# A second pair of states per tile turned on TensorE and scaled on ScalarE, and one of GpSimd's groups given to VectorE

## The chip, the cores and the metric

The kernel runs on one core of one Trainium2 chip. The metric is the device time of one execution in microseconds. A core has five engines with a queue each: TensorE (PE, with its weight loads shown apart as PEld), VectorE (DVE), ScalarE (ACT), GpSimd (POOL) and SyncE (SP, which issues most DMAs here). Each takes its instructions in order; they wait for each other through semaphores. All data is float32.

## The reference

An image tensor x of shape (4, 192, 128, 128) goes through two layers, each x + layer(group_norm(x)). Layer 1 is a convolution with fractional and ordinary Fourier transforms and is not touched. Layer 2 is a selective state-space block over the 16384 pixels of each image, read as a sequence of tokens with 192 channels. Its core, with 384 inner channels d and 16 states s:

```python
dt = softplus(einsum('blr,dr->bld', dt, dt_proj_w) + dt_proj_b)
A = -exp(A_log)                                   # (384, 16)
def step(hcar, inp):
    dt_t, B_t, C_t, u_t = inp
    dA = exp(dt_t[..., None] * A)
    hnew = hcar * dA + (dt_t * u_t)[..., None] * B_t[:, None, :]
    y_t = sum(hnew * C_t[:, None, :], axis=-1)
    return hnew, y_t
```

Ahead of it stand a layer norm, an input projection (to xs and z), a causal convolution over four tokens and silu; u is its result, and dt, B and C are projections of u. Behind it come y + u * Dp, a gate with silu(z), and an output projection.

## The kernel before

Layer 1 takes the first 1500 us. Layer 2 (`layer1` in the code, L504) cuts the 4 x 16384 tokens into 128 chunks of T = 512. A chunk has NJ = 3 tiles of 128 inner channels and NS = 16 states, taken in pairs (G = 2): NG = 8 groups per tile, 24 steps k per chunk, with tile j = k // 8 and group sg = k % 8. The loop over steps is `for pos, (n, k) in enumerate(order)` (L992); the order of the instructions is the order in which this loop writes them (a manual schedule), and each engine's queue follows it.

One state of one tile needs, for 512 tokens on 128 partitions:

- the decay exp(dt * A), by ScalarE (`decay`, L800). For groups of GpSimd it goes into a PSUM bank `op`, three states ahead (`decay_there`); for all others into one of four SBUF buffers `da`, four such states ahead (`early`);
- the input (dt * u) * B. There are three ways. GpSimd makes it for both states of a group in one operation (`inputs`, L828, tile `db`, written two steps ahead, in the queue before the `hc` of that step). VectorE makes it per state (`product`, L820), from a PSUM copy `dp` of dt * u (`dtu_copy`, L783, on ScalarE, once per tile at sg = 5) into one of the three `op` banks. Or TensorE and ScalarE do: TensorE turns dt * u so that tokens lie on partitions (`turned`, L834, four transposes of 128x128 into a `ps` bank); B is then one number per partition, so ScalarE scales it with eight activations per pair (`scale_pair`, L844, tile `dbT`, two buffers); TensorE turns it back (`turned_back`, L855, four transposes per state, into an `op` bank);
- the scan over 512 tokens, by VectorE (L869), two per step, into `h` (three buffers);
- h * C for both states, by GpSimd (L882, tile `hc`, five buffers); the sum over states by TensorE, which transposes and accumulates into `py` (`sums`, L895, three steps later; `add_skip`, L909, adds u * Dp).

At the end of a tile ScalarE copies py out (`evacuate`, L904), TensorE turns it back (`turn`, L919), and VectorE applies the gate (L924). `finish` (L933, L939) does the output projection for the chunk before.

In the same loop the *front* of later chunks goes on (`front`, a generator that advances once per step; pieces marked MID stand between the two scans of a step, pieces marked LATE behind them). For the prediction these of its lines matter: L610 to L658, the layer norm (L640 is a square root on ScalarE into `rs`, L643 its reciprocal on VectorE, L645 a transposition, L649 a copy `rows`, L653 a broadcast of the rows by TensorE, L658 the product on VectorE); L664 the input projection; L682 the convolution; L690 and L694 silu; L729 `xd`; L740, L745 and L749 dt and dt * u; L758 `bT`, the copy of B turned, which the scaling reads. Exp, silu, softplus and square root lie in different activation tables, hence ten ACT_TABLE_LOAD per chunk.

PSUM has 8 banks: three `ps`, one `dp`, three `op`, one `py`.

Which way a group goes is set by these lines:

```python
BY_POOL = ((1, 4, 7), (1, 4, 7), (1, 7))
BY_PE = 6
EARLY = 14
```

So per chunk 8 of the 24 groups are GpSimd's, 3 TensorE's and 13 VectorE's.

## Time and profile before

| | |
|---|---|
| median of 3 runs | 11592.89 us (11590.45 to 11595.39) |
| profiled execution | 11590.68 us, span 11588.6 us, mean granted clock 0.931 |
| L869 scans, DVE | 6144 in layer 2, 1263 ns each |
| L820 products, DVE | 3328, 671 ns |
| L882 hc, POOL | 3072, 2374 ns |
| L828 db, POOL | 1024, 2369 ns |
| L800 decays, ACT | 4096 of 722 ns, 2048 of 689 ns |
| L844 scaling, ACT | 3072, 371 ns (822 us busy together) |
| ACT_TABLE_LOAD of L800, ACT | 636, 1283 ns |

How to read it: durations are those of single instructions. Instructions of one engine overlap a little, so the distance from one start to the next is shorter than the duration (a 671 ns product starts 0.59 us ahead of the next instruction). Idle time stands in brackets before an instruction, with what ended it; the name given there is the last event by the profile, and where that event is long past, it was another. GpSimd's spans are rough. The granted clock is TensorE's. Steady chunks are alike, so one of them, near 6041 us, is read in detail.

### The profile page before, as it was taken

To read this page: it belongs to the slowest core of one execution; us is meant where nothing else is said; L and a number is where in the kernel's file an instruction comes from. 1 tells how busy PE (TensorE), PEld (TensorE's weight loads), DVE (VectorE), ACT (ScalarE), POOL (GpSimd) and SP (SyncE) were. 2 spreads that over 40 slices of the span, in tenths; PEclk is the share of its full clock that TensorE was granted. 3 is DMA by queue.
4 is the path that set the end of the run, shared out by engine and by line. 5 is a ranking of instruction groups with operands and counts; after the bars stand their busy time and mean duration, and the time that the engine had idled before them with its cause. 6 is when DMAs were issued, how large, how long until landed. Compare 5 with 4: busy or idle time off the path is not lost.

```text
span 11588.6 us, 153548 instructions
## 1 busy us (share of the span) xinstructions
PE 9794.3 (85%) x50570; PEld 6612.4 (57%) x50570; DVE 10751.8 (93%) x11584; ACT 8608.4 (74%) x14436; POOL 10072.1 (87%) x4598
## 2 busy tenths in 40 slices
PE   4777888888888888888888888888888888888887
PEld 2444356655656665655665665665655666566565
DVE  5565679999999999999999999999999999999999
ACT  2322168888888888888888888888888888888886
POOL 0000079999999999999999999999999999999999
PEclk8888789999999999999999999999999999999998
DMA  8787734434434434433433443443443343344343
GB/s 209 203 221 202 195 99 126 120 108 127 126 103 128 126 107 122 126 112 117 126 118 110 126 125 104 127 127 104 124 126 111 118 126 116 113 126 123 106 127 97
DMA packets 1339384, 1494.09 MB, mean 129 GB/s; under 512 B 903474, under 2 KB 954359, under 8 KB 1338071
## 3 DMA queue, kind: packets, MB, share of 16 engines
q1 hardware_dynamic: 1318102, 1421.34, 42.5%
q0 software_dynamic: 13312, 50.34, 1.4%
q10 hardware_dynamic: 7168, 12.59, 0.3%
q8 instruction: 398, 6.52, 0.2%
q14 instruction: 404, 3.30, 0.1%
HBM read 1325.19 MB, written 155.32 MB: 128 GB/s over the span
## 4 chain that ended last, share of the span: by engine, by line
DVE 32%; ACT 23%; PE 22%; issue 14%; POOL 6%; DMA 2%; DVEq 0%; SPq 0%; POOLq 0%; ACTq 0%
DVE h L869 23%; DVE op L820 7%; PE py L895 6%; ACT da L800 6%; POOL hc L882 4%; ACT op L800 4%; ACT L800 2%; ACT dbT L844 2%; PE py L909 2%; PE ps L664 2%; PE pr L471 2%; ACT dt L745 1%; POOL db L828 1%; PE ps L682 1%; PE op L855 1%
## 5 line engine op out<-in xcount | busy, mean ns | idle before, releaser
L882 POOL TENSOR_TENSOR hc<-h,bc 128x1024 f32<-128x1024 f32 x3072 | 7195.2, 2374 | 95.7 <-DVE h L869 93.7
L869 DVE TENSOR_TENSOR_SCAN h<-da,carry,op 128x512 f32<-128x512 f32 x3968 | 4932.9, 1263 | 0.0
L895 PE MATMUL py<-ident,hc 128*128 128x128 f32 x24576 | 3346.1, 283 | 604.5 <-ACT yt L904 368.3
L895 PEld LDWEIGHTS py<-ident,hc 128*128 128x128 f32 x24576 | 2941.5, 147 | 1589.7 <-issue 701.4
L800 ACT ACTIVATE da<-dt,c_A_log 128x512 f32<-128x512 f32 x4096 | 2828.1, 722 | 626.3 <-DVE h L869 620.1
L869 DVE TENSOR_TENSOR_SCAN h<-op,carry,db 128x512 f32<-128x512 f32 x1984 | 2508.4, 1264 | 86.0 <-issue 82.0
L828 POOL TENSOR_TENSOR db<-dtu,bc 128x1024 f32<-128x1024 f32 x1024 | 2425.6, 2369 | 6.3 <-DMA bc<-dbc 6.3
L820 DVE TENSOR_TENSOR op<-dp,bc 128x512 f32<-128x512 f32 x3328 | 2232.6, 671 | 32.1 <-ACT dp L783 32.1
L800 ACT ACTIVATE op<-dt,c_A_log 128x512 f32<-128x512 f32 x2048 | 1400.3, 689 | 896.4 <-DVE h L869 894.0
L664 PE MATMUL ps<-s,c_wiT 96*128 96x512 f32 x3072 | 1452.3, 595 | 2.6 <-DVE s L658 2.6
L682 PE MATMUL ps<-xs,dcw 128*128 128x512 f32 x3072 | 1424.4, 593 | 0.4 <-ACT xs L677 0.4
L933 PE MATMUL ps<-yg,c_woT 128*96 128x512 f32 x1536 | 712.1, 600 | 186.5 <-DVE xm L939 186.5
L800 ACT ACT_TABLE_LOAD x636 | 816.0, 1283 | 11.6 <-DVE h L869 0.3
L844 ACT ACTIVATE dbT<-ps,bT 128x128 f32<-128x128 f32 x3072 | 822.0, 371 | 0.0
L682 PEld LDWEIGHTS ps<-xs,dcw 128*128 128x128 f32 x3072 | 533.5, 190 | 432.3 <-issue 431.7
L664 PEld LDWEIGHTS ps<-s,c_wiT 96*128 96x128 f32 x3072 | 526.1, 191 | 379.4 <-issue 376.1
L477 POOL DMA_DIRECT2D xmid<-xt x64 | 42.6, 666 | 789.8 <-DVE xt L475 783.2
L933 PEld LDWEIGHTS ps<-yg,c_woT 128*96 128x96 f32 x1536 | 241.0, 163 | 553.8 <-issue 307.6
L633 PE MATMUL ps<-ones,xs 96*128 96x1 f32 x2048 | 292.7, 273 | 287.2 <-ACT dt L745 282.3
L909 PE MATMUL py<-ddp,u 128*128 128x128 f32 x3072 | 520.1, 326 | 0.0
L749 POOL TENSOR_TENSOR dtu<-dt,u 128x512 f32<-128x512 f32 x384 | 478.6, 1284 | 29.6 <-ACT dt L745 29.6
L909 PEld LDWEIGHTS py<-ddp,u 128*128 128x128 f32 x3072 | 487.6, 241 | 0.0
(172 smaller groups left out, 10247.2 us busy)
## 6 DMA issues: line engine op xcount, KB each, us to landing
bc<-dbc SPq DMA_DIRECT2D x1024, 1024.0 KB, 5.9
xt<-in_x SPq DMA_DIRECT2D x192, 768.0 KB, 9.6
xmid<-xt POOLq DMA_DIRECT2D x64, 768.0 KB, 7.1
xm<-xmid SPq DMA_DIRECT2D x128, 384.0 KB, 3.5
carry<-h SPq DMA_DIRECT2D x3072, 1.0 KB, 1.9
out<-xm SPq DMA_DIRECT2D x128, 384.0 KB, 3.3
d<-x ACTq DMA_DIRECT2D x64, 192.0 KB, 6.9
df<-u SPq DMA_DIRECT2D x16, 512.0 KB, 4.9
```

What stands on the lines that cost most here:

```text
L664: nc.tensor.matmul(pp, wiT[:, t, m * 128 : (m + 1) * 128], s[:, t, :], start=t == 0, stop=t == 1)
L682: nc.tensor.matmul(pc, dcw[:, j, k, :], xs[:, j, k : k + T], start=k == 0, stop=k == 3)
L749: nc.gpsimd.tensor_tensor(dtu[j], dt[j], u[j], ALU.mult)
L800: nc.scalar.activation(da, got[n]["dt"][j], AF.Exp, scale=A[:, j, st : st + 1])
L820: nc.vector.tensor_tensor(dbs[s], g["dp"], g["bc", k % NG][:, 0, q, :], ALU.mult)
L828: nc.gpsimd.tensor_tensor(db, _bc(g["dtu"][j], 1, G), g["bc", sg][:, 0], ALU.mult)
L844: nc.scalar.activation(t[:, blk, :], g["tu", j][:, blk, :], AF.Identity, scale=g["bT"][:, blk, q : q + 1])
L869: nc.vector.tensor_tensor_scan(h[:, q, :], das.pop(s), dbs.pop(s) if db is None else db[:, q, :], 0.0 if ch == 0 else g["before"][:, j, st ...
L882: nc.gpsimd.tensor_tensor(hc, h, g["bc", sg][:, 1], ALU.mult)
L895: nc.tensor.matmul(py[:, blk, :], hc[:, q, blk * 128 : (blk + 1) * 128], ident, start=first, stop=sg == NG - 1 and q == G - 1 and blk == T ...
L909: nc.tensor.matmul(got[n]["py", j][:, blk, :], got[n]["u"][j][:, blk * 128 : (blk + 1) * 128], ddp[:, j, :], start=False, stop=False, skip ...
L933: nc.tensor.matmul(po[0:CH], woT[:, j, t * CH : (t + 1) * CH], g["yg", j], start=j == 0, stop=j == NJ - 1,)
```

## The change

Group 3 of each tile joins group 6 on the way by TensorE and ScalarE. GpSimd loses group 4 of the middle tile (step 12), which VectorE then takes by products. Per chunk GpSimd has 7 groups, TensorE 6, VectorE 11. The turned dt * u of a tile serves both of its pairs; the third tile is turned twice. `TURNED` says at which step which tile is turned, `SCALED` at which step which pair is scaled: at step 0 behind the step's late pieces, elsewhere between the two scans. `bT` now holds all 16 states.

```diff
-    BY_POOL = ((1, 4, 7), (1, 4, 7), (1, 7))
-    BY_PE = 6
-    EARLY = 14
+    BY_POOL = ((1, 4, 7), (1, 7), (1, 7))
+    BY_PE = 3, 6
     MID, LATE = "mid", "late"
+
+    TURNED = {0: 0, 9: 1, 15: 2, 19: 2}
+    SCALED = {0: (0, 3), 3: (0, 6), 9: (1, 3), 11: (1, 6), 16: (2, 3), 19: (2, 6)}
...
-            g["bT"] = tp.tile([128, T // 128, G], F32, name="bT")
-            nc.scalar.copy(
-                g["bT"],
-                bt.rearrange("p (k c) -> p k c", c=128)[:, :, 96 + BY_PE * G : 96 + (BY_PE + 1) * G],
-            )
+            g["bT"] = tp.tile([128, T // 128, NS], F32, name="bT")
+            nc.scalar.copy(g["bT"], bt.rearrange("p (k c) -> p k c", c=128)[:, :, 96 : 96 + NS])
...
-            if s in turns and states[s][1] % NG != BY_PE:
+            if s in turns and states[s][1] % NG not in BY_PE:
...
-        def scale_pair(n, j):
+        def scale_pair(n, j, sg):
 
             g = got[n]
-            for q in range(G):
-                t = g["dbT", j, q] = scp.tile([128, T // 128, 128], F32, name="dbT", bufs=2)
+            for st in range(sg * G, (sg + 1) * G):
+                t = g["dbT", j, st] = scp.tile([128, T // 128, 128], F32, name="dbT", bufs=2)
...
-            if at < len(states) and states[at][1] % NG == BY_PE:
+            if at < len(states) and states[at][1] % NG in BY_PE:
...
-                if sg == BY_PE - 1:
+                if sg + 1 in BY_PE:
                     turned_back(G * (pos + 1))
...
-                if k == EARLY or sg == LAG - 1 and j < NJ - 1:
-                    turned(n, NJ - 1 if k == EARLY else j)
+                if k in TURNED:
+                    turned(n, TURNED[k])
...
                 def between():
                     go_on(parts, MID)
-                    if sg == LAG and j < NJ - 1:
-                        scale_pair(n, j)
+                    if k in SCALED and k:
+                        scale_pair(n, *SCALED[k])
...
                 go_on(parts, LATE)
-                if k == EARLY:
-                    scale_pair(n, NJ - 1)
+                if k == 0:
+                    scale_pair(n, *SCALED[k])
```

## The prediction

> **What bounds the kernel now.** First the page's busy line, then the busy time in a steady stretch of layer 2 (columns PE, PEld, DVE, ACT, POOL, granted clock, DMA share, GB/s).

> ```profile
> PE 9794.3 (85%) x50570; PEld 6612.4 (57%) x50570; DVE 10751.8 (93%) x11584; ACT 8608.4 (74%) x14436; POOL 10072.1 (87%) x4598
> ```
> ```profile
> 6000.00:8000.00 2000.00, 1732.14 (x9391) 1199.54 (x9390) 1968.67 (x2090) 1639.06 (x2772) 1985.66 (x893) 0.95 0.40 119
> ```

> GpSimd is 99.3% busy, VectorE 98.4%; ScalarE and TensorE have 18% and 13% left. Counted so, whatever leaves both saturated engines is won. So next the order of events within one chunk of 512 tokens (24 steps k of one pair of states; tiles j = k // 8). ScalarE's timeline:

> ```profile
> 2194.39 0.59 ACT L783 COPY dp<-dtu 128x512 f32<-128x512 f32 x1 [0.76 <-DVE op L820]
> ...
> 2272.90 0.59 ACT L783 COPY dp<-dtu 128x512 f32<-128x512 f32 x1 [0.76 <-POOL hc L882]
> ...
> 6041.22 0.59 ACT L783 COPY dp<-dtu 128x512 f32<-128x512 f32 x1 [0.76 <-POOL hc L882]
> ...
> 6050.80 2.12 ACT L844 ACTIVATE dbT<-ps,bT 128x128 f32<-128x128 f32 x8
> ...
> 6062.51 0.56 ACT L904 COPY yt<-py 128x512 f32<-128x512 f32 x1
> ...
> 6066.35 0.26 ACT L640 ACTIVATE rs<-ps,eps 128x4 f32<-128x4 f32 x1
> ```

> The copy of dp for the third tile (k=13) starts every 78.507 us: (6041.22 - 2272.90)/48. I call its start T0. From T0, ScalarE runs without a gap for 22.5 us (silu, softplus, four table loads, eight L844, the yt copy). VectorE and GpSimd in the same chunk:

> ```profile
> 6047.08 1.28 DVE L869 TENSOR_TENSOR_SCAN h<-op,carry,db 128x512 f32<-128x512 f32 x1 [0.67 <-issue]
> ...
> 6068.27 0.16 DVE L643 RECIPROCAL rs<-rs 128x4 f32<-128x4 f32 x1
> ...
> 6073.05 1.22 DVE L658 TENSOR_TENSOR s<-s,ps 96x1024 f32<-96x1024 f32 x1 [0.51 <-PE ps L653]
> ...
> 6106.00 1.25 DVE L869 TENSOR_TENSOR_SCAN h<-op,carry,db 128x512 f32<-128x512 f32 x1
> ```
> ```profile
> 6075.63 2.36 POOL L882 TENSOR_TENSOR hc<-h,bc 128x1024 f32<-128x1024 f32 x1 [0.59 <-DVE h L869]
> ...
> 6103.44 2.40 POOL L828 TENSOR_TENSOR db<-dtu,bc 128x1024 f32<-128x1024 f32 x1
> ```

> VectorE stands still twice per chunk, 1.2 us together: at k=15, where the scan starts 0.09 us after ScalarE's decay (6046.32 + 0.67), and at L658, which waits for the row broadcast of the front (yt, L895/L909, L664, L645, rows, L653). GpSimd waits once, for the scan after L658, and then runs 13 operations unbroken until db of group 9 is ready at about 6105.8, 0.2 us before the scan that reads it.

> So one chunk is three lengths: **A**, T0 to L658, 31.83 us, set by ScalarE and then TensorE; **B**, L658 to group 9's scan, 32.95 us, where VectorE and GpSimd end level; **C**, from there to the next T0, 13.72 us, VectorE alone. Sum 78.50.

> **The change part by part.**

> VectorE loses L820 products: groups 3, 11, 19 go to TensorE (six), group 12 comes from GpSimd (two). A product lasts 671 ns, but its start-to-start cost is 0.59 us (6040.46 to 6041.04): 4 x 0.59 = 2.34 us per chunk. The pairs fall out at k=2, k=10 and k=18, the new pair stands at k=11.

> GpSimd loses db of group 12: one of 2369 ns, 2.32 us start to start. If nothing else ended anything, a chunk would be 2.3 to 2.4 us shorter.

> ScalarE gets three more sets of eight L844. One set takes 1.99 us from its start to the next instruction (6050.80 to 6052.79); the upper end is 8 x the 371 ns mean, 2.97. I take 1.99, the same instruction in the same place. Together 6.0 us per chunk, into 78.5 - 64.4 = 14 us of idle time. The bT copy grows from 8 to 64 columns: between its 0.14 us and the 0.57 of a 128x512 copy; I take 0.2. Two decays change target (722 against 689 ns): 0.07.

> TensorE gets 24 L855 and, since the third tile is turned twice, four L834: 7 x 0.44 us = 3.1 us (0.9 each at half clock), into some 10 us of waiting. Its sums queue behind each L855, which waits for a scan; the sums release hc buffers, of which there are five, so GpSimd does not feel it. Each pair's L855 must be done before its scan. Walked through, the tightest is group 3's second (behind a convolution that waits for two xs copies, now after a set of L844), about 0.2 us early; VectorE would wait for GpSimd some steps later anyway. The second turning of tile 2 holds one of three `ps` banks until T0+23.8; L664 of the next chunk's front, which takes it, comes at 24.8 or later. Issued DMAs are the same on SP; GpSimd's queue issues none here.

> Now the three lengths.

> *A.* The set for group 19 replaces the old one of tile 2, only behind xd instead of before it: yt stays at T0+21.3. The set for group 22 now stands at k=19, right behind yt and in front of bT, the table load and rs. Before, rs was done at T0+25.4 and VectorE asked at T0+27.05. After: 20.05 (end of the L800 load, 6061.27 - 6041.22) + two decays 1.24 + yt 0.47 + set 1.99 + two decays 1.24 + bT 0.2 + load 1.29 + rs 0.3 = T0+26.8. VectorE, 1.17 us earlier through k=18, asks at T0+25.85 and stands still for about 1 us. That gain is gone. Then k=21 (2.36), L924 (0.58), a scan (1.18): VectorE asks for L658's operand at T0+31.1. Meanwhile ScalarE does load 1.3, two decays 1.24, dp 0.6, rows 0.2 (T0+30.1), and TensorE L653, 1.1: T0+31.3. A shrinks from 31.8 to 31.3.

> *B.* The scan behind L658 ends at T0+33.6; 13 GpSimd operations at 2.319 us ((6105.78 - 6075.63)/13) are the same 13 as before. db of group 9 comes at T0+64.0, its scan at 64.15. VectorE would be there at 63.1 (pair at k=2 gone) and waits at groups 7 and 9. B keeps 32.8.

> *C.* The pair saved at k=10 returns at k=11: 13.72 as before.

> Sum 77.95, 0.55 us less than 78.507. Over 127 intervals 70 us. The profiled execution took 11590.7 us (span 11588.6), 2 us under the median 11592.9: 11590.7 - 70 = 11521 us.

> The floor, with nothing late in A: GpSimd's hc of k=12 ends at T0+1.8 at the earliest (its scan ends with C); seven operations later, at 18.1, come the three L749 (3.7 us), 18 operations more bring db of group 9 at 63.5, plus C: 77.3. So at most 1.2 us per chunk, 11437.

> [...] Granted clock around the yt copy:

> ```profile
> 6060.00:6061.00 1.00, 1.00 (x9) 1.00 (x9) 1.00 (x2) 1.00 (x1) 1.00 (x2) 0.68 0.00 0
> ...
> 6067.00:6068.00 1.00, 1.00 (x9) 0.99 (x8) 1.00 (x2) 0.99 (x2) 1.00 (x1) 0.91 1.07 274
> ```

> Half clock lasts from 6060.36 to 6067.18 (by the shares 0.68 and 0.91 of these slices), 6.83 us, in every chunk at the same place (T0+19.1), and it slows exactly the work behind yt. In early chunks it began at T0+20.5 (1664.0) and the chunk took 79.19; T0+19.33 (1899.5) gave 78.61, T0+19.23 (1978.0) gave 78.56. 78.507 is 23 times 3.413, half the slow time: the chunk is locked to the clock's own period.
> [...]

> **Rivals.**
> *Full gain:* the balance decides, 76.1 us per chunk, 11285 to 11437 us. For it: 99.3% and 98.4%. Against: A and C hold nothing that the change shortens.
> *Locked again:* the slow time stays behind yt and A stretches until the chunk is 23 periods: 11590, no change. For it: the lock; against: the two L855 of group 19 fill the gap before L633, whose 2.4 us of waiting precede the slow time.
> *ScalarE too late (slower):* the set at k=19 delays rs, and VectorE's reciprocal stands in order before the scans, so A grows one for one. From 0.55 us beyond my figure the change loses; with 2.97 per set A is 1 us longer, 0.4 us per chunk over before: 11645.

> **How the numbers follow.** Forecast case 0.48, full gain 0.07, locked 0.18, ScalarE too late 0.27. The likeliest gives 11521, its own range 11475 to 11565. Leaving out the full gain and the worse part of the slower case, 11450 to 11640. Within 0.2% (23 us), what a measurement here can tell from no change: 0.18; faster 0.55; slower 0.27.

> **What would show it.** L820 at 2816 instead of 3328, L828 at 896, L844 at 6144. A new wait of the reciprocal on L642's rs of about 1 us per chunk; VectorE waiting for GpSimd's db at groups 7 and 9; GpSimd idle 2 us per chunk, before hc of k=12 and k=22; ScalarE near 91% busy. dp copies at k=13 77.9 us apart and no longer at a fixed place of the slow clock. I am wrong if rs or an L855 is later than walked here, or if the chunk stays at 78.507.

## The result and the profile after

The changed kernel takes 11584.31 us (median, 11580.53 to 11592.76), the kernel before, beside it, 11588.52 us; the ratio is 0.9997, 95% interval 0.9988 to 1.0006. That is no change, where 11521 was forecast. The profiled execution has a span of 11590.8 us.

The page's busy line, and the steady stretch of layer 2 (columns PE, PEld, DVE, ACT, POOL, granted clock, DMA share, GB/s):

```profile
PE 10615.0 (92%) x54154; PEld 7007.7 (60%) x54154; DVE 10503.1 (91%) x11072; ACT 9334.7 (81%) x17508; POOL 9823.7 (85%) x4470
```
```profile
6000.00:8000.00 2000.00, 1895.96 (x10107) 1279.08 (x10105) 1919.13 (x1988) 1784.58 (x3381) 1936.76 (x868) 0.96 0.41 120
```

The work did move. VectorE fell from 98.4% to 96.0%, GpSimd from 99.3% to 96.8%, ScalarE rose from 82% to 89%. None of it became time. What VectorE waited for in 4000 to 8000 us, 51 chunks (us in total, times, longest):

```profile
DVE rs L645 <- ACT rs L642: 58.3, 51, 2.0
DVE h L869 <- PE op L855: 45.1, 85, 1.3
DVE h L869 <- issue: 34.8, 51, 0.9
DVE h L869 <- POOL db L827: 14.6, 57, 0.8
DVE s L660 <- PE ps L655: 8.4, 51, 0.3
```

Before, two waits filled this list, at k=15 ("issue") and at L658:

```profile
DVE h L869 <- issue: 33.3, 50, 1.0
DVE s L658 <- PE ps L653: 27.1, 51, 1.0
```

The new ones, for rs, for op and for db, are 2.3 us per chunk together, as long as the four products that VectorE lost. One chunk, the lines that answer to those of the prediction; first ScalarE's timeline, then VectorE's and GpSimd's:

```profile
6047.48 0.59 ACT L782 COPY dp<-dtu 128x512 f32<-128x512 f32 x1 [0.20 <-issue]
...
6068.86 0.56 ACT L904 COPY yt<-py 128x512 f32<-128x512 f32 x1
6069.32 2.17 ACT L843 ACTIVATE dbT<-ps,bT 128x128 f32<-128x128 f32 x8
...
6074.13 0.26 ACT L642 ACTIVATE rs<-ps,eps 128x4 f32<-128x4 f32 x1
...
6125.91 0.59 ACT L782 COPY dp<-dtu 128x512 f32<-128x512 f32 x1
```
```profile
6074.43 0.18 DVE L645 RECIPROCAL rs<-rs 128x4 f32<-128x4 f32 x1 [0.99 <-ACT rs L642]
6078.91 1.22 DVE L660 TENSOR_TENSOR s<-s,ps 96x1024 f32<-96x1024 f32 x1 [0.16 <-PE ps L655]
6095.11 1.28 DVE L869 TENSOR_TENSOR_SCAN h<-da,carry,op 128x512 f32<-128x512 f32 x1 [0.84 <-PE op L855]
6111.86 1.28 DVE L869 TENSOR_TENSOR_SCAN h<-op,carry,db 128x512 f32<-128x512 f32 x1 [0.17 <-POOL db L827]
6120.41 1.28 DVE L869 TENSOR_TENSOR_SCAN h<-da,carry,op 128x512 f32<-128x512 f32 x1 [0.20 <-PE op L855]
```
```profile
6109.43 2.40 POOL L827 TENSOR_TENSOR db<-dtu,bc 128x1024 f32<-128x1024 f32 x1
```

T0 is 6047.48. A ends at L660, 6078.91: 31.43. Group 9's scan starts at 6111.86, so B is 32.95, and C, to 6125.91, is 14.05. The sum is 78.43. Over many chunks it is not: from 6047.48 to 11386.02 there are 68, of 78.508 us in the mean, the 78.507 of before. Two things have to be explained, then: why a chunk is 78.43 and not 77.95, and why the mean is 78.51 and not 78.43.

The second shows when chunks are set in a row (start of the chunk, its length, then where slow-clock stretches begin, counted from T0, and how long they last; worked out from the dp copies and the granted clock):

```
4712.68  78.43   15.6: 3.4 us   32.7: 3.4 us
4791.11  78.46   15.7: 3.4 us   32.7: 3.4 us
4869.57  78.42   15.7: 3.4 us   32.8: 3.4 us
4947.99  78.21   15.8: 3.4 us
5026.20  79.18   12.7: 6.8 us   33.2: 3.4 us
5105.38  78.42   15.4: 3.4 us   32.5: 3.4 us
```

The slow stretches of the steady chunks last 3.413 us or a whole multiple of it (4000 to 11300 us: 158 of 3.41 and 14 of 6.83 here; 6 of 3.41, 90 of 6.83 and 3 of 13.65 before), and the starts of all stretches in a trace, 283 here and 181 before, lie whole multiples of 3.4133 us apart, to 0.02 us; I call 3.413 us a window of the clock. 23 windows are 78.507. A chunk of 78.42 is 0.085 short of that, so the stretches move later in the chunk, from T0+15.4 to T0+15.8. Then the window ahead is slow too, the clock is slow for 6.8 us from T0+12.7, and that chunk takes 79.18. After that it begins anew, and the mean stays at 23 windows. That the windows hold the mean there is read from such rows; the runs that take the slow time away, below, test it.

The slow time also bears on the first question. The chunk at 4947.99 has no stretch near T0+32 and takes 78.21. In the 14 chunks of this kind between 4000 and 11300 us (of 93), C is 13.81 and not 14.05: TensorE reaches group 11's L855 at T0+72.05 there, and at T0+72.29 in the chunks with the stretch, since it comes out of the stretch late and has 0.4 us of idle time on the way to catch up, against 1.4 us in the 14. The wait of 0.20 us at 6120.41 above is what VectorE sees of it; in the 14 chunks it is 0.01. So some 0.25 of the 78.43 is slow time that lies 40 us ahead of the wait.

### The profile page after: what moved, and what is told of

It reads as the page before. It is cut to its first block, busy times and chain, and to the rows that moved or that the text cites. A ratio compares the mean times of both kernels' runs of the same rounds, so it can differ in the third digit from the quotient of the medians.

```text
span 11590.8 us, 163663 instructions
## 1 busy us (share of the span) xinstructions
PE 10615.0 (92%) x54154; PEld 7007.7 (60%) x54154; DVE 10503.1 (91%) x11072; ACT 9334.7 (81%) x17508; POOL 9823.7 (85%) x4470
## 4 chain that ended last, share of the span: by engine, by line
PE 35%; DVE 28%; ACT 23%; issue 11%; DMA 2%; POOL 1%; DVEq 0%; SPq 0%; ACTq 0%; POOLq 0%
DVE h L869 18%; PE ps L666 8%; ACT da L799 7%; PE py L895 7%; PE ps L684 6%; DVE op L819 5%; PE ps L933 3%; ACT dbT L843 3%; ACT L799 3%; PE op L855 3%; ACT op L799 2%; PE pr L471 2%; ACT s L612 2%; ACT L692 1%; ACT L642 1%
## 5 line engine op out<-in xcount | busy, mean ns | idle before, releaser
L882 POOL TENSOR_TENSOR hc<-h,bc 128x1024 f32<-128x1024 f32 x3072 | 7195.0, 2366 | 342.6 <-DVE h L869 338.2
L869 DVE TENSOR_TENSOR_SCAN h<-da,carry,op 128x512 f32<-128x512 f32 x4216 | 5227.0, 1267 | 115.2 <-PE op L855 110.9
L895 PEld LDWEIGHTS py<-ident,hc 128*128 128x128 f32 x24576 | 2963.8, 147 | 787.8 <-issue 716.3
L895 PE MATMUL py<-ident,hc 128*128 128x128 f32 x24576 | 3360.5, 283 | 25.7 <-POOL hc L882 12.4
L799 ACT ACTIVATE da<-dt,c_A_log 128x512 f32<-128x512 f32 x4352 | 3008.5, 728 | 356.9 <-DVE h L869 349.4
L869 DVE TENSOR_TENSOR_SCAN h<-op,carry,db 128x512 f32<-128x512 f32 x1736 | 2203.2, 1269 | 116.7 <-issue 83.6
L827 POOL TENSOR_TENSOR db<-dtu,bc 128x1024 f32<-128x1024 f32 x896 | 2146.2, 2395 | 6.4 <-DMA bc<-dbc 6.4
L819 DVE TENSOR_TENSOR op<-dp,bc 128x512 f32<-128x512 f32 x2816 | 1897.8, 674 | 32.1 <-ACT dp L782 32.1
L843 ACT ACTIVATE dbT<-ps,bT 128x128 f32<-128x128 f32 x6144 | 1656.8, 379 | 11.8 <-PE ps L833 11.6
L799 ACT ACTIVATE op<-dt,c_A_log 128x512 f32<-128x512 f32 x1792 | 1222.3, 683 | 548.0 <-DVE h L869 546.5
L855 PE MATMUL op<-ident,dbT 128*128 128x128 f32 x6144 | 1084.1, 297 | 102.2 <-DVE h L869 78.3
L855 PEld LDWEIGHTS op<-ident,dbT 128*128 128x128 f32 x6144 | 795.1, 152 | 528.5 <-ACT dbT L843 149.1
L742 PE MATMUL ps<-xd,c_dtT 12*128 12x512 f32 x768 | 443.6, 662 | 99.4 <-ACT dbT L843 76.0
```

What stands on the lines that cost most here:

```text
L799: nc.scalar.activation(da, got[n]["dt"][j], AF.Exp, scale=A[:, j, st : st + 1])
L819: nc.vector.tensor_tensor(dbs[s], g["dp"], g["bc", k % NG][:, 0, q, :], ALU.mult)
L827: nc.gpsimd.tensor_tensor(db, _bc(g["dtu"][j], 1, G), g["bc", sg][:, 0], ALU.mult)
L843: nc.scalar.activation(t[:, blk, :], g["tu", j][:, blk, :], AF.Identity, scale=g["bT"][:, blk, st : st + 1],)
L855: nc.tensor.transpose(db[:, blk * 128 : (blk + 1) * 128], t[:, blk, :], ident)
L869: nc.vector.tensor_tensor_scan(h[:, q, :], das.pop(s), dbs.pop(s) if db is None else db[:, q, :], 0.0 if ch == 0 else g["before"][:, j, st ...
```

## The experiments

Each is timed beside the kernel before, and ratios are to it. "Undisturbed" means the commonest chunk in the trace without a long slow stretch in A.

### Which group GpSimd gives up

```diff
-    BY_POOL = ((1, 4, 7), (1, 7), (1, 7))
+    BY_POOL = ((1, 7), (1, 4, 7), (1, 7))
```

> The changed kernel, but the group that GpSimd gives up is group 4 of the first tile (k=4) and not of the middle tile (k=12). All engine totals are those of the changed kernel. Theory of three lengths (A: T0 to the front's product, B: from there to group 9's scan, C: from there to the next T0): GpSimd's unbroken row in B is 12 operations and not 13, VectorE has 1.17 us more there and sets it at 32.9 us; C loses the products of group 12 (1.17 us) but the scan of group 11 then waits 0.6 us longer for TensorE's transposes; A stays 31.4. Sum about 78.0 us per chunk, 11535 us (11500 to 11560). Engine totals: no difference to the changed kernel, 11584. Clock lock: the chunk stays at 78.507 on average, 11588.

Measured: 11583.96 us, ratio 0.9997 (0.9988 to 1.0006). Undisturbed 78.44, every sixth or seventh chunk longer, mean 78.50. Not even the undisturbed chunk fell: C fell by 0.34 and B rose by as much, to 33.29 (32.96 in the chunks without a stretch near T0+32). Its trace shows what took the two products' place, TensorE's turned state of group 11:

```profile
6189.86 1.28 DVE L869 TENSOR_TENSOR_SCAN h<-da,carry,op 128x512 f32<-128x512 f32 x1 [1.06 <-PE op L855]
```

### The two parts of the change alone

TensorE and ScalarE's part alone is the changed kernel with the old line:

```diff
-    BY_POOL = ((1, 4, 7), (1, 7), (1, 7))
+    BY_POOL = ((1, 4, 7), (1, 4, 7), (1, 7))
```

> The second pair on TensorE and ScalarE alone; GpSimd keeps all eight groups. Three lengths: A 31.4, B 32.95 (GpSimd's row unchanged), C loses the products of group 12 and gains a longer wait for the transposes, 13.4; but GpSimd has 77.9 us of work per chunk, so 78.0 to 78.4 us, 11525 to 11575. Engine totals: GpSimd bound as before, 11588. ScalarE too late: above 11600, with waits of the reciprocal well over 1 us.

Measured: 11589.58 us, ratio 1.0000 (0.9991 to 1.0010). Chunks of 77.8, 78.9, 78.7 and 78.6 by turns. Four of them are 92 windows, so the mean is 78.50 again, with a quite different shape: in the three longer ones A is 32.3 to 32.5, with 6.8 us of slow clock ahead of yt.

GpSimd's group alone is the kernel before with one line changed:

```diff
-    BY_POOL = ((1, 4, 7), (1, 4, 7), (1, 7))
+    BY_POOL = ((1, 4, 7), (1, 7), (1, 7))
```

> The kernel before with one of GpSimd's groups (k=12) given to VectorE and nothing else. Three lengths: C grows by a pair of products, 1.17 us, A and B stay: 79.7 us per chunk, 11735 us. Engine totals: VectorE 78.3 us busy and 1.2 us of waits, 79.5 us, 11715. Clock lock: if the chunk is held at a multiple of the clock's 3.413 us it would stay at 78.507; with VectorE longer than that the lock must break.

Measured: 11725.2 us, ratio 1.0119 (1.0102 to 1.0136). Undisturbed 79.29 = A 31.41, B 32.96, C 14.92. C grew by 1.20, which is two products of 0.59; A and B kept their length although GpSimd had one operation less. The op that GpSimd gave up lay in the length that VectorE alone sets. The mean is 79.64, three chunks being 70 windows.

### Filling TensorE's time ahead of the slow stretch, in the kernel before

```diff
-            for j in range(NJ):
+            for j in [*range(NJ)] * 3:
                 rows = slice(32 * j, 32 * j + RANK)
                 nc.tensor.matmul(d[j], dtT[rows, :], xd[rows, :], start=True, stop=True)
```

> The kernel before with the three dt projections (L740) computed three times over into the same banks, 12 more passes of 512 columns per chunk, which fill TensorE's gap ahead of L633; the result is the same. Clock lock: no slow time behind the yt copy, so the row broadcast is no longer late, the chunk leaves 78.507 and falls to what GpSimd (77.9 us busy) and VectorE (77.1 plus 0.7 of waiting for a decay) allow: 77.9 to 78.1 us, 11520 to 11550 us, with slow time gone or elsewhere. If the clock has no part in it: 78.5 us and 11588, or more by the added work.

Measured: 11604.87 us, ratio 1.0014 (1.0004 to 1.0023). It went the wrong way: some chunks of 78.10, some of 80.1 to 81.8, and for the most part the old 78.507. This miss led to the cause. The granted clock in two windows in a row, and TensorE in the first of them:

```profile
6060.12:6063.53 3.41, 3.40 (x24) 1.72 (x25) 3.41 (x4) 3.39 (x6) 3.41 (x2) 1.00 0.19 27
6063.53:6066.94 3.41, 3.41 (x19) 3.41 (x18) 3.41 (x5) 3.38 (x5) 3.41 (x3) 0.50 0.04 0
```
```profile
6060.13 2.85 PE L740 MATMUL ps<-xd,c_dtT 12*128 12x512 f32 x18 [1.59 <-ACT xd L729]
```

TensorE is busy for 3.40 of the 3.41 us of a window, and the clock is halved behind it. What fills the window are matmuls of 12 rows. A little less of them, and the clock stays whole, with TensorE as busy as before:

```profile
7084.13:7087.54 3.41, 3.41 (x25) 1.73 (x26) 3.41 (x4) 3.39 (x6) 3.41 (x2) 1.00 0.16 20
7087.54:7090.96 3.42, 2.75 (x25) 2.52 (x24) 3.42 (x5) 3.39 (x5) 3.42 (x3) 1.00 0.06 5
```
```profile
7083.98 2.85 PE L740 MATMUL ps<-xd,c_dtT 12*128 12x512 f32 x18 [1.59 <-ACT xd L729]
```

The 12-row matmuls begin 0.15 us ahead of this window and have 2.70 us of it; the rest are L895's transposes. The trace holds 75 windows with over 2.6 us of 12-row matmuls (4000 to 11300 us, at full clock, all but one busy throughout). The 13 with less than 2.80 us of them are followed by full clock, those with more by half clock, and at 2.80 (to 0.01) both occur. So in this run it is not idle time that halves the clock.

### Convolution behind the turned state, and both moves together

In the changed kernel, a `yield LATE` moves the convolution matmuls of the first and third tile behind L855 in TensorE's queue:

```diff
+            yield LATE
             c0 = psum()
             conv(0, c0, 0)
...
             conv(2, c2, 0)
             yield
+            yield LATE
             conv(2, c2, 1)
```

> The changed kernel with two pieces of the front's convolution (first half for tile 0 at k=2, second half for tile 2 at k=10) moved on TensorE's queue behind the transposes of groups 3 and 11 that stood behind them. Three lengths: the wait of group 11's scan (0.28 us with its restart) goes out of C; the wait at group 3 goes too but GpSimd's row in B still sets the time there. 78.42 falls to 78.14, about 35 us under the changed kernel, 11550. Engine totals or clock lock: no difference, 11584.

Measured: 11581.91 us, ratio 0.9994 (0.9985 to 1.0002). Chunks of 78.13 and 78.90 by turns, two of them 46 windows. The undisturbed chunk fell by 0.3 as the lengths said (C is 13.75); the time did not.

With group 4 of the first tile given up as well:

> The same two pieces moved and the group taken from GpSimd at k=4 and not at k=12. Three lengths: A 31.4, B 32.9 set by VectorE, C 12.8: 77.2 us per chunk, 11420 us (11400 to 11460). Engine totals: as the changed kernel, 11584. Clock lock: 11588.

Measured: 11495.19 us, ratio 0.9918 (0.9905 to 0.9932). Undisturbed 77.08, with others of 78.3 (A 32.6 in place of 31.42, with 6.8 us of slow clock in it). Five chunks are 114 windows, so the mean is 77.81. The mean has left 78.507, but 0.7 us per chunk is still lost to slow time.

### The third tile's second pair taken back

The changed kernel with group 19 on VectorE again and the set for group 22 back at k=14:

```diff
-    BY_PE = 3, 6
+    BY_PE = (3, 6), (3, 6), (6,)
...
-    TURNED = {0: 0, 9: 1, 15: 2, 19: 2}
-    SCALED = {0: (0, 3), 3: (0, 6), 9: (1, 3), 11: (1, 6), 16: (2, 3), 19: (2, 6)}
+    TURNED = {0: 0, 9: 1, 14: 2}
+    SCALED = {0: (0, 3), 3: (0, 6), 9: (1, 3), 11: (1, 6), 14: (2, 6)}
```

> The changed kernel with the second pair in the first two tiles only; the third tile is turned once at k=14 as before, and VectorE takes group 19 by products again, 1.17 us more for VectorE, 2 us less for ScalarE per chunk. Three lengths: A is 31.4 either way (the reciprocal no longer waits 1.1 us, VectorE uses that time for the products), so the same time within 0.2%, 11584, plus the slow clock, which may come back behind the yt copy and lock the chunk at 78.507. Engine totals: VectorE 76.0 us busy, GpSimd 75.6, no difference if GpSimd sets it, up to 1.1 us per chunk (140 us) slower if VectorE does.

Measured: 11589.72 us, ratio 1.0001 (0.9992 to 1.0010). All chunks 78.507, as before. Its A of 31.73 holds slow time, so it says nothing on what the added set costs; the last experiment below does.

### Narrow matmuls made wide

The question is now whether the narrow matmuls are the cause, so they are made wide, one kind after the other. In the chunk of the changed kernel read above, the slow stretch at T0+15 stands behind the dt matmuls (12 of 128 rows), the one at T0+32 behind the spreading of 1/std (4 rows). The two pairs of windows, and dt matmuls in the first one (the trace shows each of these matmuls as two instructions, x2 below):

```profile
6059.49:6062.90 3.41, 2.83 (x11) 1.24 (x12) 3.41 (x4) 3.41 (x9) 3.41 (x2) 1.00 0.05 0
6062.90:6066.31 3.41, 3.30 (x17) 2.91 (x15) 3.41 (x5) 3.38 (x5) 2.83 (x3) 0.50 0.06 5
6076.55:6079.97 3.42, 2.33 (x19) 2.02 (x18) 3.26 (x4) 3.42 (x7) 3.42 (x3) 1.00 0.80 265
6079.97:6083.38 3.41, 3.41 (x7) 1.35 (x6) 3.41 (x5) 2.82 (x5) 3.19 (x2) 0.50 0.78 231
```
```profile
6059.35 1.12 PE L742 MATMUL ps<-xd,c_dtT 12*128 12x512 f32 x2 [0.18 <-DVE s L622]
6061.05 1.12 PE L742 MATMUL ps<-xd,c_dtT 12*128 12x512 f32 x2 [0.58 <-ACT dbT L843]
```

First the dt matmuls alone get all rows of xd and weights that are zero outside the 12, so the sums are the same:

```diff
+        dtz = cp.tile([128, NJ, 128], F32, name="dtz")
+        nc.vector.memset(dtz, 0.0)
+        for j in range(NJ):
+            rows = slice(32 * j, 32 * j + RANK)
+            nc.sync.dma_start(out=dtz[rows, j, :], in_=w["dtT"][rows, :])
...
-                rows = slice(32 * j, 32 * j + RANK)
-                nc.tensor.matmul(d[j], dtT[rows, :], xd[rows, :], start=True, stop=True)
+                nc.tensor.matmul(d[j], dtz[:, j, :], xd, start=True, stop=True)
```

> The changed kernel, with the three dt matmuls (128x512 outputs, until now fed by 12 of TensorE's 128 rows) given all 128 rows of xd and weights that are zero outside the 12; sums, order and durations as before. Ahead of every slow stretch of TensorE near T0+15 stands a window of 3.41 us that holds these matmuls; in it TensorE was busy for 2.8 us of 3.41, in the run with the dt matmuls done three times even for all 3.41, and the clock was halved all the same. Theory 'narrow matmuls': TensorE's clock is halved after a window in which too little of the array worked, and 12 rows count for little. Then the stretch near T0+15 goes, the one near T0+32 (behind the 4-row matmuls) stays, and the chunk is at most the undisturbed 78.42: 11530 to 11578 us. Rival 'idle time': the gaps of 0.18 and 0.58 us between the dt matmuls make it. Then all stays: both stretches, 78.51 a chunk, 11584 us.

Measured: 11581.88 us, ratio 0.9997 (0.9988 to 1.0006). The time said "idle time", the trace said "narrow matmuls". The window of the wide dt matmuls, with the same waits between them, and the one behind it:

```profile
6044.87:6048.28 3.41, 2.46 (x7) 0.81 (x6) 3.41 (x4) 3.41 (x11) 3.41 (x3) 1.00 0.12 20
6048.28:6051.70 3.42, 3.00 (x22) 2.23 (x20) 3.42 (x5) 3.39 (x5) 3.15 (x2) 1.00 0.05 0
```

Busy for 2.46 us, the clock stays whole; with 12 rows 2.83 us did not do. The stretch near T0+15 is gone from all 93 chunks between 4000 and 11300 us. But the one near T0+32, which should have stayed, is left in 8 of them only, though its 4-row matmuls are as they were, and in 62 chunks others stand near T0+20, behind the next narrow matmuls: the sums of squares, one column wide:

```profile
6051.70:6055.11 3.41, 3.17 (x30) 2.94 (x28) 3.41 (x5) 3.38 (x5) 3.41 (x3) 1.00 0.11 8
6055.11:6058.52 3.41, 2.56 (x14) 2.19 (x12) 3.41 (x5) 3.41 (x12) 3.41 (x3) 0.50 0.12 21
```
```profile
6052.67 1.84 PE L640 MATMUL ps<-ones,xs 96*128 96x1 f32 x16
```

Chunks are 78.2 three times and 79.35 once, 92 windows again.

Next, in the same kernel, the 1/std matmuls with all rows too:

```diff
-        sel = cp.tile([4, 4, CH], F32, name="sel")
-        nc.vector.tensor_copy(sel, _bc(ident[0:4, 0:4], 2, CH))
+        sel = cp.tile([128, 4, CH], F32, name="sel")
+        nc.vector.tensor_copy(sel, _bc(ident[:, 0:4], 2, CH))
+        rows = cp.tile([128, 128], F32, name="rows")
+        nc.vector.memset(rows, 0.0)
...
-            rows = tp.tile([4, 128], F32, name="rows")
-            nc.scalar.copy(rows, rt[0:4, 0:128])
+            nc.scalar.copy(rows[0:4, :], rt[0:4, 0:128])
```

> As the run before, and the four matmuls that spread the rows of 1/std (4 of 128 rows until now) get all 128 rows too, with zeros in the other 124. Theory 'narrow matmuls': no chunk of layer 2 shows a clock under 1.00 any more, there is nothing left for the loop to lock to, and all chunks have one length, that of the three lengths of the prediction as they were measured, 78.4 us, or less where the slow stretches had stood in a length: 11500 to 11576 us. Rival 'idle time': both stretches stay, 11584 us. Rival 'locked by something else': the clock is full, but the chunk is still 78.507: 11584 us.

Measured: 11579.59 us, ratio 0.9995 (0.9987 to 1.0004). Chunks of 78.2, 78.2 and 79.15: 69 windows for three. "No chunk shows a clock under 1.00" missed: 73 of 93 chunks still have slow time. None of it stands behind the widened matmuls; each of the 73 stretches follows a window with 1.71 to 1.84 us of one-column matmuls.

The same two in the version with both moves:

> The version with group 4 given up in the first tile and the conv matmuls behind the turned products (11495 us, chunks of 77.08 and 78.3 by turns, the longer ones those with 6.83 us of slow clock), and in it the dt matmuls and the 1/std matmuls with all 128 rows. Theory 'narrow matmuls': all chunks are 77.08 or a little less: 11380 to 11410 us. Rival 'idle time': 11495 us.

Measured: 11420.22 us, ratio 0.9861 (0.9847 to 0.9874). Chunks 77.10, now and then 78.1. The expected 11410 was missed by those.

Then the kernel before, with a third filling, the sums of squares 96 columns wide:

```diff
-                        var[:, q : q + 1], sq[:, t, q * 128 : (q + 1) * 128], ones[0:CH, 0:1],
+                        var[:, 96 * q : 96 * q + 96], sq[:, t, q * 128 : (q + 1) * 128], ones[0:CH, :],
...
-            nc.scalar.activation(rs, var[:, 0:4], AF.Sqrt, bias=eps, scale=1.0 / C)
+            nc.scalar.activation(rs, var[:, 0:384:96], AF.Sqrt, bias=eps, scale=1.0 / C)
```

> The kernel before, with all 128 rows for the dt and the 1/std matmuls, and with the sums of squares made 96 columns wide instead of one (column 0 is used; a 96x1 output took 2.24/16 = 0.14 us, so it should last about as long). Its slow stretch stood behind a window with 1.50 us of these one-column matmuls and 1.9 us idle. It gives the length of the kernel before without the lock, which no run has shown. Theory 'narrow matmuls': if 1.5 us of full matmuls hold the clock (1.9 us of transposes did, in the trace of before), no slow stretch is left and the chunk is what the three lengths have without it: 77.5 to 78.4, 11470 to 11575 us. Rival 'idle time': the stretch stays, the chunk is 23 windows, 78.507: 11588 us.

Measured: 11533.08 us, ratio 0.9954 (0.9941 to 0.9968). Without one instruction moved, the kernel before gains 54 us, most of what the change was to bring. "No slow stretch is left" missed: 48 of 93 chunks still have one, of 3.4 us and later (T0+22), where it costs little: chunks are 78.13 with it and 78.05 without. A is 31.41 to 31.46 either way, in place of 31.83. Its steady stretch, and VectorE's waits in 4000 to 8000 us:

```profile
6000.00:8000.00 2000.00, 1723.85 (x9444) 1180.15 (x9443) 1978.15 (x2103) 1656.88 (x2793) 1996.93 (x899) 0.99 0.40 118
```
```profile
DVE h L874 <- issue: 33.4, 49, 1.0
DVE h L874 <- POOL db L833: 3.9, 7, 0.9
DVE s L664 <- PE ps L659: 1.5, 2, 0.8
```

GpSimd is 99.8% busy, so with its work as it is the chunk has almost nothing left to lose; L658's wait, 27.1 us in the kernel before, is 1.5.

Last, the changed kernel and the version with both moves, with all three fillings:

> The changed kernel with all three fillings: 128 rows for the dt and the 1/std matmuls, and the sums of squares 96 columns wide. The only slow stretches left in the run with two fillings stood behind windows with 1.40 to 1.84 us of one-column matmuls, busy for 3.05 and 3.17 us of 3.41. Theory 'narrow matmuls': they go too, every chunk is the 78.2 of that run's undisturbed ones (31.46 + 32.89 + 13.86), and the mean is no longer 78.507: 11540 to 11553 us. Since the kernel before takes 11533 (78.09 a chunk) with the same fillings, the change by itself then costs 0.1 us a chunk, some 14 us. Rival 'another place takes over': a longer chunk every few chunks brings the mean back to 78.50: 11580 us.

> The version with group 4 given up in the first tile and the conv matmuls behind the turned products, with all three fillings (11420 us with two, chunks of 77.10 and now and then 78.0). Theory 'narrow matmuls': no chunk of 78 is left, mean 77.1, 11400 to 11412 us. Rival 'another place takes over': 11420 us or more.

Measured: 11546.22 us, ratio 0.9960 (0.9947 to 0.9974), and 11404.28 us, ratio 0.9841 (0.9828 to 0.9855). The first has a mean chunk of 78.176, the second 77.068, neither a simple number of windows. Both lie in the range of 'narrow matmuls', no slow stretch is left in the steady chunks of either, and the rival falls. The second is the fastest version of this study and beats both kernels. The changed kernel's steady stretch and its waits:

```profile
6000.00:8000.00 2000.00, 1827.93 (x10147) 1228.42 (x10145) 1929.96 (x1997) 1795.61 (x3395) 1942.28 (x872) 1.00 0.40 117
```
```profile
DVE rs L652 <- ACT rs L649: 51.5, 51, 1.6
DVE h L874 <- issue: 34.6, 51, 0.9
DVE h L874 <- POOL db L832: 34.6, 96, 0.7
DVE s L666 <- PE ps L661: 8.7, 51, 0.3
```

So the change by itself, with the slow time gone (changed kernel) or nearly free of cost (kernel before), brings nothing: 78.18 against 78.09 in the traces, 11546 against 11533 us (the two intervals overlap, so of a loss only the traces speak). VectorE's busy time per chunk fell from 77.24 to 75.44 (1978.15/2000 x 78.088 and 1929.96/2000 x 78.176), and its waits rose from 0.76 to 2.5 us.

### The added set ahead of the square root

In that last version of the changed kernel, the set for group 22 is done by one activation per state:

```diff
+                if (j, sg) == (2, 6):
+                    nc.scalar.activation(
+                        t, g["tu", j], AF.Identity, scale=g["bT"][:, 0, st : st + 1]
+                    )
+                    continue
                 for blk in range(T // 128):
```

> The changed kernel with the three fillings, in which the set for group 22 at k=19, the one that stands ahead of the square root rs, is done by one activation of 512 columns per state instead of four of 128 (with one factor for all four, so that part of the computation is changed: group 22 is scaled by the B of one token block only). One 128x512 activation of ScalarE starts 0.57 to 0.62 us ahead of the next, so the set takes 1.2 us instead of 1.99. Theory 'ScalarE's chain sets A': VectorE stands still for 1.0 us for rs and 0.16 us for the broadcast, so A falls by nearly all of the 0.75, to 30.7, the chunk to 77.45, 11440 to 11465 us. Rival 'VectorE or another wait is next in A': A stays at 31.44 and the time at 11546 us.

Measured: 11516.04 us, ratio 0.9937 (0.9923 to 0.9951), chunks of 77.96. Both theories had a part of it. A fell by 0.92, to 30.52, about what the set was shortened by (1.15 us from its start to the next instruction, 2.01 before; I had estimated 0.75 to 0.8); B grew from 32.89 to 33.62. VectorE's waits:

```profile
DVE h L879 <- POOL db L832: 67.9, 153, 0.7
DVE h L879 <- issue: 34.6, 51, 0.9
DVE s L666 <- PE ps L661: 8.9, 52, 0.3
DVE h L879 <- PE op L865: 1.6, 4, 0.6
DVE rs L652 <- ACT rs L649: 1.4, 2, 0.7
```

The wait for rs is gone and the wait for GpSimd's db doubled. ScalarE's set does hold A, as the prediction walked it, but GpSimd stands 0.2 us behind it for A and B together (64.14 against 64.32).

## Why the prediction was wrong

The three lengths, undisturbed, in all kernels that decide something:

| | A | B | C | sum | mean chunk |
|---|---|---|---|---|---|
| before | 31.83 | 32.95 | 13.72 | 78.50 | 78.507 |
| before, three fillings | 31.41 | 32.95 | 13.72 | 78.08 | 78.088 |
| forecast | 31.3 | 32.8 | 13.72 | 77.95 (the terms add up to 77.82) | 77.95 |
| changed | 31.43 | 32.95 | 14.05 | 78.43 | 78.508 |
| changed, three fillings | 31.43 | 32.89 | 13.87 | 78.19 | 78.176 |
| both moves, three fillings | 31.44 | 32.95 | 12.69 | 77.08 | 77.068 |
| quick set | 30.52 | 33.62 | 13.84 | 77.98 | 77.954 |

The step that failed is the one that put slow time in the changed kernel at nothing: the prediction argued that the added L855 fill TensorE's gap ahead of L633, so that the slow time behind yt goes, and the sum has no term for slow time anywhere else. It did go from behind yt, and A came out nearly as forecast. But in all 93 chunks between 4000 and 11300 us there is other slow time: in 14 of them 6.8 us from T0+13, which makes A 32.2 to 32.4, and in 78 of them 3.4 us near T0+32, which makes C 14.05 in place of 13.81. The wider range, 11450 to 11640, holds the measured time by its width and not by its likeliest case.

- **The balance.** "Whatever leaves both saturated engines is won" was kept out of the forecast by the walk through the lengths, and rightly: VectorE and GpSimd lost 2 us each and wait that much more.
- **A.** The walk was good: rs late by 1 us at k=20 (1.14 in the mean of the trace), L660 at T0+31.43 against 31.3. What misled is the 31.83 it was set against. Of that, 0.42 was slow clock behind yt: with the fillings the kernel before has 31.41. (The 6.83 us stand at T0+19 in 81 of its 93 chunks between 4000 and 11300 us, not in every one.) The change took VectorE's work out of A and put ScalarE's set in its place, 31.43; the 0.5 us that I booked as won was the clock's, and the changed kernel pays it elsewhere.
- **B.** It is 32.95, as before. The forecast's 32.8 was a slip: it had read 32.95 itself, and its own times give 32.85 (64.15 less 31.3). 13 operations of GpSimd took 2.33 us apiece, start to start, in place of 2.319; its db lasts 2395 ns where it lasted 2369.
- **C.** The mis-sized term: 14.05 in place of 13.72. The new pair of group 11 was walked as in time; its second scan waits 0.20 us for L855, which stands behind the convolution in a queue that slow time near T0+32 has set back. At full clock C is 13.87: that scan still starts 0.68 us behind the product ahead of it, where 0.59 is usual, which is 0.1 of the 0.15 left; the rest is not accounted for. With the convolution moved behind L855 C is 13.75.
- **The tightest L855.** Group 3's second was walked as 0.2 us early. Its scan waits 0.84 us (6095.11 above), again behind the stretch near T0+32; in the 14 chunks without that stretch it waits 0.16. B did not grow by it, since GpSimd's db, for which VectorE then waits less, sets its end.
- **GpSimd's group.** I priced it as 2.32 us off a saturated engine. The run with this part alone shows that group 12 lies in C, where VectorE sets the pace: two products more, 1.20 us longer, nothing won. Given up in the first tile, together with the conv move, C is 12.69.
- **The rival *Locked again*** had 0.18 and came true in time and mean chunk, though not by its wording: the slow time did not stay behind yt, it went to two other places. So far its number was right by luck. What I held against it, that a filled gap before L633 would take the slow time away, asked for one place only; there are three kinds of narrow matmuls in a chunk, and slow time followed windows with each of them: 12 rows at 6059.49, 4 rows at 6076.55, and one column at 6051.70 in the run with wide dt matmuls. I also took a lock for one fixed place. The mean stays at 78.5 as well with chunks of different lengths by turns.
- ***Full gain*** and ***ScalarE too late*** fell: rs was as late as walked, not later, and no balance decided.
- **Of what would show it,** the counts, the waits for rs and for db at groups 7 and 9, and ScalarE's share (89% for 91%) came. The dp copies stayed 78.5 apart, and with them came both signs of being wrong: an L855 later than walked, and the mean chunk at 78.507.
- **The gap as the cause.** That the 2.4 us of waiting before L633 make the slow time behind yt was read from their order alone, and no run shows it: a window whose longest gap was 0.58 us (6059.49 in the changed kernel), and one with no gap at all (6060.12 in the run with the dt matmuls three times over, busy for 3.40 of 3.41 us), were followed by half clock.

So both questions have an answer. A chunk is 78.43 since the change's own gain at full clock is nil (78.18 against 78.09, the two kernels with all fillings) and slow time near T0+32 adds 0.25. The mean is 78.51 since narrow matmuls halve the clock in some windows and stretch some chunks (shown by its going away when all three kinds are made wide: the mean is 78.176, and no slow stretch is left in the steady chunks). How far a given chunk length is drawn to a number of windows, and why before, with one place, stays there without moving, was not worked out.

## What to carry to other kernels

Here the period of a steady loop was a whole number of the 3.413 us that its trace shows in the slow clock (78.507, or 23.00), a measured length held slow time (0.42 us of A), and a forecast gain of 0.55 us did not show. So make this division before costing an edit: where it comes out whole, look for the windows that are followed by half clock, and fill them first. Then cut the loop into stretches by what bounds each, and ask of every instruction removed in which stretch it stood: the same product or group is worth 1.2 us in one and nothing in the next. A forecast for an undisturbed step is tested against undisturbed steps of both kernels, and not against a mean.

## What the runs showed of the hardware

```profile
6056.95:6060.36 3.41, 1.50 (x14) 1.50 (x14) 3.41 (x5) 3.38 (x5) 3.41 (x3) 1.00 0.04 0
6101.32:6104.73 3.41, 2.13 (x17) 1.67 (x15) 3.41 (x5) 1.02 (x2) 3.41 (x2) 1.00 0.04 0
```

A window with wide dt matmuls kept the clock although all but 12 rows of their weights are zero. No single amount of wide work marks the border. Full clock followed 1.65 us in the kernel before (4227.40, convolution for the most part). Half clock followed 2.06 us in the kernel before with three fillings, where 96-column sums of squares make up 1.64 of it:

```profile
8457.46:8460.87 3.41, 2.06 (x19) 1.82 (x18) 3.41 (x5) 3.38 (x6) 3.41 (x4) 1.00 0.04 0
8460.87:8464.28 3.41, 2.86 (x14) 2.89 (x15) 3.41 (x5) 2.86 (x5) 3.41 (x3) 0.50 0.04 0
```

What in a window decides stays open. Making a 12-row matmul 128 rows deep cost nothing: in the first run that did so the two instructions of one lasted 1.12 us together, as those of L742 do above.
